# Graph layer and feed-forward block on one core: where the edge keys, the attention rows, the router constants and a comparison table are placed

## The chip, the cores and the metric

The kernel runs on one core of a Trainium2 chip. The metric is the device time of one execution in microseconds (us); lower is better. The core has five engines that each take their instructions in order: PE (matrix multiply; PEld is its weight load), DVE (vectors), ACT (activations and copies), POOL (GpSimd) and SP (which here only issues transfers). Transfers are issued by SP, ACT and POOL, and a transfer that has to wait holds up what stands behind it on its issuing engine.

## The reference

The inputs are x of 1250 nodes by 768, and 41250 edges (src, dst), sorted by dst, with one loop edge for each node among them. Cut to what matters:

```python
n_nodes = x.shape[0]
loops = jnp.arange(n_nodes)
src = jnp.concatenate([edge_index[0], loops]); dst = jnp.concatenate([edge_index[1], loops])

def _gat_layer(x, W, a_src, a_dst, b, src, dst, n_nodes):
    h = x @ W
    e = leaky_relu((h @ a_src)[src] + (h @ a_dst)[dst], 0.2)
    m = segment_max(e, dst);  w = exp(e - m[dst]);  z = segment_sum(w, dst)
    alpha = w / z[dst]
    return segment_sum(h[src] * alpha[:, None], dst) + b

x = x + gat2(relu(gat1(layernorm(x))))
y = layernorm(x)                       # then a feed-forward block:
y = y + attention(ln(y))               # 12 heads of 64, over 1250 rows
x = x + y + moe(ln(y))                 # 8 experts, the best 2 for each row
```

## The kernel before

The kernel turns the edges into a dense matrix of counts, `cnt` (how often the edge from node s to node d occurs), so that a graph layer becomes matrix products over 10 tiles of 125 nodes. It goes through these stages: edge lists and the first layer's projection (to 72 us), counting (to 136 us), two graph layers, attention over 12 heads, the output projection with the router, and the experts.

**The edge lists.** The 41250 edges lie as 125 rows of 330. Their lists `ri` are loaded, and DVE makes one number of each edge, `key` = dst * 1250 + src. The keys are stored to memory (`keys`, with a short `tail` behind them), because the next steps gather from there by computed rows. From the first key of each row, `find_rows` works out in which row each node's edges begin (`begun` on DVE, ten small products on PE, `row` and `edges` on DVE). For each tile t of 125 nodes, `gather_row(t)` fetches that row of keys for each node (`kr`, an indirect transfer issued by POOL, three buffers: LEAD = 3), and `first_edges(t)` counts on DVE how many keys of it are smaller, which gives the position of the node's first edge, and has POOL gather a window of 64 keys from there (`win`). When all ten windows are there, DVE turns them into node numbers, PE sums how many were found (`psum`) and transposes them (`pl`).

**The tiles of x**, beside the edge lists: `spread(t)` loads a tile where it hasn't been loaded yet (four buffers, so tile t waits until tile t - 4 is transposed; even tiles are issued by SP, odd ones by ACT) and takes its statistics on DVE and the root on ACT; `normal(t)` makes the reciprocal and the offset on DVE and scales the tile on ACT; `columns(t)` transposes it on PE in two halves, which ACT copies to `xnT`. `project` multiplies a tile with the layer's weights `gw` (24 matmuls, then ACT copies `h`). `vector(n)` takes n of the 12 products of `gw` with the attention vectors (`scr`, on DVE; the result is `wa`). The vectors are loaded as rows repeated on all partitions (`rep`). `attention_terms` multiplies `wa` with `xnT` on PE (`pe`).

**What sets the order.** Within `tc.manual_schedule`, PE, DVE and POOL keep the order in which the program writes their instructions; ACT and SP are ordered by the scheduler. Instructions outside of such a block are placed by the scheduler where it finds room, unless `tc.keep_in_program_order` pins them. The router's constants (`beyond`, `used`, `start`, `slot`, `before`, `number`, `ones`; lines 781 to 814) are written after attention, are not pinned, and were placed by it in the first 26 us: `ones` on DVE at 1 us, six instructions on POOL behind the first three row gathers, and the comparison that makes `before` a triangle (L812) on DVE behind tile 3's statistics.

**The queues at the start.** SP issues ri (dst), tiles 0 and 2, and the weights `gw` (L112); ACT issues ri (src), `tail`, tiles 1 and 3, and then the keys' store (L233). Of the eight semaphores that count the transfers of SP and ACT, each is used again by a later transfer, which waits for the earlier one: so the weights' issue waits for tile 0, and the store of the keys for tile 1 and for `key`.

**Counting** (L402 to L413): for each of 25 groups of edge positions, DVE compares the source nodes with the table `lane` (`ohp`) and, five times in all, the targets with the table `upto` (`ohj`); PE multiplies the two, and ACT copies the counts. `upto` is made by an iota on POOL (L252).

## Time and profile before

| | |
|---|---|
| median of 3 runs | 1541.51 us (1534.36 to 1543.46) |
| the profiled execution | 1542.12 us, of which the span is 1540.3 us |
| PE busy | 1454.5 us (94%) |
| DVE busy | 797.8 us (52%) |
| ACT busy | 597.6 us (39%) |
| POOL busy | 431.6 us (28%) |
| the chain that ended last | PE 71%, DVE 9%, issue 8%, DMA 5%, ACT 4%, POOL 2% |

Busy time is an average over stages with different limits. The stage that the change is about takes 72 us of 1540, and in it PE is busy for about half of the time: of three stretches of 20 us from the start, PE works 3.6, 12.2 and 18.0 us. A row of the list of waits names the instruction that stood still, what ended its wait, the total in us, how often, and the longest. A row of the chain is start, length, and what the end of the kernel goes back to at that time; "issue" is time in which nothing that the profile shows was waited for. A row of the timeline is start, busy time, engine, line, operation, output and input. The clock in the stretches is what PE was granted, 1.00 being full.

### The profile page before, as it was taken

What the parts mean: (1) busy time and instruction counts of PE and PEld (TensorE: products, weight loads), DVE (VectorE), ACT (ScalarE), POOL (GpSimd) and SP (SyncE); (2) the same over time, 40 slices, a digit from 0 to 9 for tenths busy, and PEclk for the clock granted to TensorE, in tenths of its full rate; (3) what the DMA queues carried; (4) which work ended last, traced back from release to release, by engine and by line L of the source; (5) the groups of instructions that cost most, each with busy time, mean ns of one, the idle gap of its engine ahead of it and who ended that gap; (6) DMA issues with size and microseconds to landing.
All of it is one profiled execution on the core that took longest, in us unless ns stands there. A gap on an engine that the chain in (4) does not pass through costs nothing.

```text
span 1540.3 us, 15938 instructions
## 1 busy us (share of the span) xinstructions
PE 1454.5 (94%) x5981; PEld 782.3 (51%) x5981; DVE 797.8 (52%) x1285; ACT 597.6 (39%) x950; POOL 431.6 (28%) x287
## 2 busy tenths in 40 slices
PE   3889999999999999999999999999988997799998
PEld 2476655555555555553344444434333665466665
DVE  4698633205326740117877877877888665011111
ACT  3321503202414621215655655655656354212121
POOL 5300000000000002004764664664666222122222
PEclk9956999999999999999999999999999997899999
DMA  6200010000021118940000000000030333755644
GB/s 182 66 1 32 11 72 0 0 11 2 1 81 55 56 44 339 407 176 20 1 21 1 21 0 21 1 21 1 0 101 1 131 119 113 288 169 179 219 153 142
DMA packets 48847, 125.49 MB, mean 81 GB/s; under 512 B 6103, under 2 KB 22680, under 8 KB 48768
## 3 DMA queue, kind: packets, MB, share of 16 engines
q1 hardware_dynamic: 30540, 55.04, 10.8%
q0 software_dynamic: 12688, 57.10, 9.8%
q10 hardware_dynamic: 5540, 12.31, 2.7%
q8 instruction: 48, 0.79, 0.2%
q14 instruction: 31, 0.25, 0.1%
HBM read 71.30 MB, written 57.60 MB: 84 GB/s over the span
## 4 chain that ended last, share of the span: by engine, by line
PE 71%; DVE 9%; issue 8%; DMA 5%; ACT 4%; POOL 2%; POOLq 0%; SPq 0%; ACTq 0%; DVEq 0%
PE pagg L525 12%; PE ph L201 9%; PE st L659 8%; PE pav L703 7%; PE pk L622 5%; PE pv L638 5%; PE phe L988 5%; PE poe L997 5%; PE pq L622 4%; DMA xd<-yn,slot 2%; DVE sT L689 2%; PE pc L409 2%; PE pe L190 2%; PE po L846 2%; PE ptr L140 1%
## 5 line engine op out<-in xcount | busy, mean ns | idle before, releaser
L695 POOL TENSOR_TENSOR acc<-acc,sT 125x834 f32<-125x834 f32 (+1 forms) x139 | 272.9, 1963 | 10.9
L525 PE MATMUL pagg<-h,wt 125*125 125x385 f32 (+1 forms) x800 | 262.7, 486 | 0.4 <-DVE wt L518 0.4
L668 DVE TENSOR_TENSOR most<-most,st 125x834 f32<-125x834 f32 (+1 forms) x144 | 147.0, 1021 | 105.3 <-ACT sT L662 101.9
L525 PEld LDWEIGHTS pagg<-h,wt 125*125 125x125 f32 x800 | 147.5, 187 | 106.0 <-DVE wt L518 2.7
L689 DVE TENSOR_TENSOR sT<-sT,mb 125x834 f32<-125x834 f32 (+1 forms) x180 | 174.1, 1016 | 22.9 <-PE mb L684 22.9
L690 ACT ACTIVATE sT<-sT 125x834 f32<-125x834 f32 (+1 forms) x180 | 158.4, 900 | 49.8 <-DVE sT L689 49.4
L662 ACT COPY sT<-st 125x834 f32<-125x834 f32 (+1 forms) x180 | 151.5, 847 | 51.4 <-PE st L659 46.4
L659 PE MATMUL st<-qk 64*125 64x417 f32 (+1 forms) x720 | 164.5, 556 | 3.9 <-DVE most L668 3.8
L703 PE MATMUL pav<-sT,v 125*64 125x417 f32 (+1 forms) x720 | 151.1, 532 | 9.3 <-ACT sT L690 9.3
L600 POOL MEMSET zero<- 128x772 f32 x1 | 0.7, 741 | 519.2 <-PE ptr L140 519.2
L695 POOL TENSOR_TENSOR acc<-sT 125x834 f32<-125x834 f32 (+1 forms) x18 | 35.3, 1963 | 276.0 <-ACT sT L690 276.0
L659 PEld LDWEIGHTS st<-qk 64*125 64x125 f32 x720 | 56.6, 184 | 99.1 <-DVE most L668 42.9
L703 PEld LDWEIGHTS pav<-sT,v 125*64 125x64 f32 x720 | 42.5, 136 | 106.0 <-issue 44.5
L997 PE MATMUL poe<-we,hT 128*128 128x384 f32 x264 | 88.8, 486 | 0.0
L622 PE MATMUL pq<-yT,wqk 128*128 128x417 f32 (+1 forms) x216 | 88.1, 534 | 0.0
L846 PE MATMUL po<-wp,aT 128*125 128x384 f32 x240 | 87.5, 498 | 0.0
L988 PE MATMUL phe<-xT,we 128*128 128x384 f32 (+1 forms) x288 | 86.6, 460 | 0.0
L1001 DVE SCALAR_TENSOR_TENSOR sofar<-poe,weight,sofar 128x768 f32<-128x768 f32 x25 | 25.4, 1018 | 116.3 <-PE poe L997 116.2
L622 PE MATMUL pk<-yT,wqk 128*128 128x417 f32 (+1 forms) x216 | 84.0, 526 | 0.0
L201 PE MATMUL ph<-gw,xnT 128*125 128x384 f32 x240 | 82.6, 504 | 0.0
L638 PE MATMUL pv<-wv,yT 128*125 128x384 f32 x240 | 79.9, 490 | 1.4 <-issue 1.4
L201 PE MATMUL ph<-gw,x1T 128*125 128x384 f32 x240 | 78.6, 487 | 0.0
(219 smaller groups left out, 1734.6 us busy)
## 6 DMA issues: line engine op xcount, KB each, us to landing
xd<-zero POOLq DMA_DIRECT2D x8, 3860.0 KB, 47.4
we<-in_L_ffn_W_dram SPq DMA_DIRECT2D x16, 1152.0 KB
xr<-xd SPq DMA_DIRECT2D x25, 386.0 KB
gw<-in_L_gnn_W_dram SPq DMA_DIRECT2D x2, 2304.0 KB
wqk<-in_L_ffn_Wqkv_dram SPq DMA_DIRECT2D x12, 384.0 KB
xres<-in_x_dram SPq DMA_DIRECT2D x10, 375.0 KB
xsd<-xres ACTq DMA_DIRECT2D x10, 375.0 KB
wv<-in_L_ffn_Wqkv_dram SPq DMA_DIRECT2D x1, 2304.0 KB
```

The costliest lines, as they stand in the source:

```text
L201: nc.tensor.matmul(po[:, s, :DH], xT[:, c, t * T:(t + 1) * T], w[:, c, s * DH:(s + 1) * DH], start=(c == 0), stop=(c == DC - 1))
L525: nc.tensor.matmul(po[:, s, :DH + s], ws[j][:, (d - d0) * T:(d - d0 + 1) * T], h[:, j, s * DH:(s + 1) * DH + s], start=(j == 0), stop=(j = ...
L622: nc.tensor.matmul(pq[:, :w], wqk[:, c, i, :], yT[:, c, c0:c0 + w], start=(c == 0), stop=(c == DC - 1))
L638: nc.tensor.matmul(pv[:T, s, :DH], yT[:, c, t * T:(t + 1) * T], wv[:, c, s * DH:(s + 1) * DH], start=(c == 0), stop=(c == DC - 1))
L659: nc.tensor.matmul(st[:T, i, :w], self.qk[r, 1, j * T:(j + 1) * T], self.qk[r, 0, self.c0:self.c0 + w], start=True, stop=True)
L662: nc.scalar.copy(s[:, :, :w], st[:T, :, :w])
L689: nc.vector.tensor_tensor(s[:, :, :w], s[:, :, :w], self.mb[:T, :, :w], ALU.subtract)
L690: nc.scalar.activation(s[:, :, :w], s[:, :, :w], AF.Exp)
L695: nc.gpsimd.tensor_tensor(self.acc[:, :, :w], prev[:, :, :w], s[:, :, :w], ALU.add)
L703: nc.tensor.matmul(self.pav[r, :w], v[:, j, hd0:hd0 + HD], s[:, i, :w], start=(j == 0), stop=(j == NT - 1))
L988: nc.tensor.matmul(ph[:, :n * P], w1[:, c, f * P:(f + 1) * P], xT[:, c, :n * P], start=(c == 0), stop=(c == DC - 1))
L997: nc.tensor.matmul(po[:, d, :DH], hT[:, f, s * P:(s + 1) * P], w2[:, f, d * DH:(d + 1) * DH], start=(f == 0), stop=(f == FC - 1))
```

## The change

Five edits:

1. **The keys' store** is issued by SP, pinned in program order between the x tiles and the weights; the weights' load stands behind it (and is written out, without the helper `load_big_weight`).
2. **The rows of attention vectors** of the first layer are issued by SP, and a first `vector(1)` at the head of the manual schedule issues both without taking a product: they stand right behind the weights. The second layer's rows stay on ACT.
3. **The tiles** 4 to 9 are spread, normalized and transposed one step of the loop later: `spread(t + 2)` for t from 2 to 7 in place of `spread(t + 3)` for t from 1 to 6, and the spread comes ahead of `first_edges(t)`. So between the first and the second projection PE transposes one tile (was two), between the second and the third three, and after the third two (was one).
4. **The table `upto`** is made by POOL after the first three row gathers, not ahead of them.
5. **The router's constants** are pinned to their place in the program, after attention: the six POOL instructions stand ahead of the memsets of `yn`, and `ones` and `before` on DVE after the last division of attention. `tail` and the odd tiles of x stay on ACT.

On SP's queue the order is now: ri, tiles 0 and 2, keys, weights, two rows, tiles 4, 6, 8.

```diff
@@ attention_vectors
             def load(a):
                 rep = pool.tile([P, D], F32, tag="rep", name="rep", bufs=bufs)
-                tc.keep_in_program_order(nc.scalar.dma_start(
+                tc.keep_in_program_order((nc.sync if bufs > 1 else nc.scalar).dma_start(
                     rep, bass.AP(tensor=a.tensor, offset=a.offset, ap=[[0, P], [1, D]])))
                 return rep
 
             reps = [load(a) for a in (a_src, a_dst)[:bufs]]
+            if bufs > 1:
+                yield None
@@ edge lists
-            gw = load_big_weight(gW1, "gw1")
...
-            nc.scalar.dma_start(keys[0:E].rearrange("(p e) -> p e", p=T), key)
+            tc.keep_in_program_order(nc.sync.dma_start(keys[0:E].rearrange("(p e) -> p e", p=T), key))
+            gw = wpool.tile([P, DC, D], F32, tag="w", name="gw1")
+            tc.keep_in_program_order(nc.sync.dma_start(gw, gW1.rearrange("(c p) f -> p c f", p=P)))
...
             upto = ep.tile([P, 2 * NT, 5 * PG], BF16, name="upto")
-            nc.gpsimd.iota(upto, pattern=[[1, 2 * NT], [0, 5 * PG]], base=1, channel_multiplier=0,
-                           allow_small_or_imprecise_dtypes=True)
...
             with tc.manual_schedule(engines=fixed):
+                vector(1)
                 pk = find_rows()
...
                 for t in range(LEAD):
                     gather_row(t)
+                nc.gpsimd.iota(upto, pattern=[[1, 2 * NT], [0, 5 * PG]], base=1, channel_multiplier=0,
+                               allow_small_or_imprecise_dtypes=True)
...
                 for t in range(NT):
+                    if 2 <= t <= 7:
+                        spread(t + 2)
                     first_edges(t)
                     if t + LEAD < NT:
                         gather_row(t + LEAD)
                     if t % 3 == 0 and t // 3 < EARLY:
                         project(xT, gw, h, gpo, [t // 3])
-                    if 0 < t <= 6:
-                        spread(t + 3)
                     vector(0 if t < 3 else 1 if t < 5 else 2)
-                    if 0 < t <= 6:
-                        normal(t + 3)
-                        columns(t + 3)
+                    if 2 <= t <= 7:
+                        normal(t + 2)
+                        columns(t + 2)
@@ router constants
+    pin = tc.keep_in_program_order
...
-    nc.gpsimd.iota(beyond, pattern=[[REG, NE], [P, NR]], base=CAP - NOWHERE, channel_multiplier=0,
-                   allow_small_or_imprecise_dtypes=True)
+    pin(nc.gpsimd.iota(beyond, pattern=[[REG, NE], [P, NR]], base=CAP - NOWHERE, channel_multiplier=0,
+                   allow_small_or_imprecise_dtypes=True))
...
-    nc.gpsimd.iota(before, pattern=[[1, T]], base=0, channel_multiplier=-1,
-                   allow_small_or_imprecise_dtypes=True)
-    nc.vector.tensor_scalar(before, before, 0.0, None, ALU.is_gt)
+    pin(nc.gpsimd.iota(before, pattern=[[1, T]], base=0, channel_multiplier=-1,
+                   allow_small_or_imprecise_dtypes=True))
+    pin(nc.vector.tensor_scalar(before, before, 0.0, None, ALU.is_gt))
...
```

## The prediction

> **What bounds the kernel now.** I read the page first: PE is busy for 94% of the span and the chain that ended last is PE for 71% of it. The diff touches three places: the edge lists in the first 72 us, the counting loop that reads the table `upto`, and the router 1200 us later. From 78 us on the kernels issue the same instructions in the same order except for eight small ones near the router, so I looked for what ends last in the first 72 us. First the list of waits for 0 to 130 us (engine, line and operation, what ended the wait: total us, times, longest):
>
> ```profile
> POOL kr L278 <- issue: 12.8, 10, 10.2
> PE ptr L140 <- ACT xnT L298: 12.4, 5, 10.2
> ...
> ACT xn L319 <- DVE less L318: 11.3, 6, 8.6
> ...
> DVE before L812 <- POOL before L810: 9.2, 1, 9.2
> ...
> DVE good L374 <- PE psum L372: 4.1, 1, 4.1
> DVE scr L181 <- DMA rep<-in_L_gnn_att_src_dram: 4.1, 1, 4.1
> ```
>
> Four engines stand still at one time, for 9 to 10 us. The chain, in order of time (start us, us, what), says why:
>
> ```profile
> 9.81 9.59 DMA keys<-key
> 19.44 0.97 issue
> 20.41 1.38 POOL kr L278
> ...
> 25.61 0.20 POOL before L810
> 25.83 0.23 DVE before L812
> 26.06 0.08 DVE rstd L316
> 26.17 0.17 DVE less L318
> 26.36 1.03 ACT xn L319
> ...
> 31.59 8.68 PE ph L201 x24
> ...
> 63.02 8.56 PE pe L190 x24
> 71.58 0.33 PE psum L372 x2
> 71.94 0.17 DVE good L374
> ```
>
> The keys' store takes 9.59 us; POOL's three row gathers wait for it; the router's iota `before` stands behind the gathers on POOL; DVE, in order, waits for that iota with tile 3's rstd behind it; ACT can't scale the tile, PE can't transpose it. A router constant holds up the graph layer. PE then runs without a long gap from 31.4 to 71.5.
>
> The timeline shows one more thing at the start:
>
> ```profile
> 7.69 2.51 POOL L252 IOTA upto<- 128x2500 bf16 x1
> ...
> 8.29 1.98 DVE L243 TENSOR_SCALAR node<-node 125x10 f32<-125x10 f32 x1
> ```
>
> A 125x10 operation took 1.98 us beside the iota; `row`, of the same shape, took 0.17. The Trainium skill's "SBUF — State Buffer", "Who interferes with whom", says that a GpSimd operation and a VectorE tensor_scalar in a two-port mode lock each other out, whole instructions at a time; this pair looks like it, and by it all of the 1.8 us would go.
>
> **Step 1, router constants out of the way** (tiles and lists are counted from 0). DVE loses the wait of 9.2 us. Tile 3's variance is done at 16.5 (stats from 15.19, 1.02 + 0.21), ACT's root follows by 16.9, rstd and less by 17.2; ACT scales tile 2 from 16.79 to 17.82 and can scale tile 3 at 17.85, not 26.36: 8.5 us earlier. With `upto` gone from 7.69, `node` costs 0.17 and `begun` about 0.98 (twice the 0.49 of jf, 128x625), so both end near 9.45, not 10.92. The x tile that the statistics wait for is there by 9.47 (the weights' issue waits for the same tile, and went then). So these come 0 to 1.3 us earlier; I take 1.0. The first projection starts at 31.4 - 9.5 = 21.9.
>
> What hid behind the stall is the weights' load. It was issued at 9.47; the transfer rate stands at 362 to 417 GB/s from 12 to 17 us and falls at 17.5, so it ended near 17.8. Now the issue comes about 0.4 us later (one SP issue more), with 165 KB of keys ahead and 3 x 165 KB of gathers beside it, 1.6 us at 400 GB/s: it lands near 19.8. That is 2 us of cover; each microsecond past 21.9 would cost one.
>
> **Step 2, the keys.** The store moves from ACT, where it followed the weights' issue by 0.34 us, to SP ahead of them. It waits there for the key (8.05) and the first x tile, so it goes at about 9.5. Its landing is not in the trace: at best 2.9 us after the issue (the shortest landing of any gather of these lists), at worst 9.6, as before. I take 4 us, near the low end: the first x tiles are nearly through (1.57 MB of 1.87 MB moved by 9.0), and 165 KB need 1.3 us at the 131 GB/s with which the 125-row loads at 140 to 146 us run. So POOL starts the first gather at 9.5 + 4 + 1.0 (its lag in the chain) = 14.5. Gathers landed 3.9 to 7.6 us after their start, median 4.3; beside the weights I take 5.5. Call F the time at which DVE can begin on the first list: F = 20.0, within 17.3 (9.5 + 2.9 + 1.0 + 3.9) and 27.7 (9.5 + 9.6 + 1.0 + 7.6).
>
> A rule speaks against this step. The Trainium skill's "DMA: Bandwidth & Descriptors", "Queues, rings and completion order", says each DMA engine alternates between queues packet by packet. By it the store on ACT's queue needn't have waited for the weights on SP's, and would now take as long: F would be 26. The 9.59 us, 1.5 us past the weights' end, look like a queue in order, and I go by them.
>
> **Step 3, the loop over edge lists.** DVE takes it in order. From F it has two lists, then a tile's statistics (1.27), list (0.68), up to two attention products (0.98 each), rstd and less (0.28) in turn. Gather t+3 starts behind the window gather t (1.5 us each on POOL) and lands 4.3 us later, so list 3 stands at F + 7.9 and list 6 at F + 18.3; tile 8 is normal at F + 21.6, and ACT has scaled it at F + 22.7. `upto` (2.51) now sits on POOL between the third gather (done near 19) and the first window gather, due at F + 0.7 = 20.7; that is nearly free, 0.8 us late at worst here. The rows of attention vectors, issued right behind the weights, remove DVE's 4.1 us for `rep`. That wait wasn't on the path (DVE itself waited 4.1 us for psum at the end).
>
> **Step 4, what is late next.** The lead of the x tiles drops by one: between the first and second projection stands one tile's transposes, not two, and tile 9's load can be issued only after the second projection. With the first projection's start S = 21.9, that one ends at S + 17.3 (8.7 + 0.8 + 7.8). ACT then copies h (0.8), evicts tile 5, scales tile 8 (1.03), evicts tile 6 and issues the load in two parts around tile 7, done near S + 22.8. Before, it was issued at 43.83 and 45.68, S + 14. It lands 2.5 to 3.8 us later (a tile waited for at 34.3 had its issue end at 30.5): S + 26. From its statistics to the last product DVE needs 9.0 us (51.29 to 62.32 before, less two products that now stand earlier): S + 35. The last of six terms and the second chunk's six follow, 0.71 each: S + 40. That equals PE's own 40.1 us (31.4 to 71.5), so the tail uses up its slack and costs 0 to 1. ACT's turn for tile 8 ends at S + 20.2. If list 6 is late, F + 22.7 passes that and all of this moves; that is so when F passes 19.4, and F = 20.0 costs 0.6.
>
> **Step 5, constants at the router.** Two DVE instructions (0.17 + 0.23) come after the last division at 1201.6; DVE idles 1.02 us at 1208.09 for po, which takes them. POOL's six (1.1 together) come before a memset at 1193.3, and POOL idles 4.2 us after it. Nothing; uncovered, 0.4 and 1.1. The load and rows on SP delay no one: SP's next x tile waits for PE at 16.5 anyway.
>
> **Sum.** psum now starts at 71.5; then at 21.9 + 40.1 + 0.6 + 0.4 = 63.0: 8.5 us. The order after that is the same, so it stays to the end. The profiled execution took 1542.1 (span 1540.3 and 1.8 around it), close to the median of the runs, 1541.5: 1542.1 - 8.5 = **1533.6**.
>
> **The rivals.**
> *The gathers take the wait over* (0.22). If the store stays slow or gathers are starved, F = 23 to 27, and psum starts at about F + 42.5 (22.7, and the 19.8 from S + 20.2 to S + 40). For: the store's own 9.59 us beside the weights. Against: it is now ahead of them. Gain 2 to 6: 1536 to 1540.
> *The change doesn't do what it says* (0.08). The weights land after 29, or the order of queues means nothing: gain under 2, 1540 to 1542.
> *Slower* (0.06): the first gather, on POOL's queue, lands only after weights and attention rows and tiles, past 29.0 us, where F + 42.5 passes 71.5. One microsecond each; at 34 it makes 1547. Against it: weights, rows, keys, gathers and the rest of the tiles are 4.1 MB, done by 22 us at 400 GB/s.
> *More* (0.08): PE's clock, 0.50 from 76 to 144 us, drops in PE's wait at 73 to 79. With a warm PE the counting stage (58.7 us) is left to DVE's 25 x 1.90 + 5 x 1.46 = 54.8: another 3.9, 1529 to 1530. The same wait remains, so I doubt it.
>
> **How the numbers follow.** My forecast has 0.56, 7 to 10 us. The three runs before spread over 9 us, so the median of the runs after may lie 4 off on its own. From the largest gain (10) less 5 for that, the range reaches down to 1526; up to 1542 it takes in the first two rivals. A measurement of this kernel tells about 1% (15.4 us) from no change. No case here reaches that alone; forecast and *more* with a lucky median give faster 0.10, the slower rival with an unlucky one slower 0.05, within 1% 0.85.
>
> **What would show it.** In the new profile: no wait of DVE for `before` in the first 72 us; `node` near 0.2 us; the first gather at 14 to 15 and the first list at 18 to 22; projection one at 21 to 23; psum at 62 to 65. Wrong: a keys landing still near 19; projection one waiting for the weights; DVE standing for kr or for x tile 9 by more than 6 us; a different clock in the counting stage.

## The result, and the profile after

The changed kernel takes 1539.82 us in the median of 14 runs (1537.19 to 1541.68), the kernel before 1542.26 us in 14 runs taken beside it (1534.36 to 1543.98): ratio 0.9989, 95% interval 0.9979 to 0.9999. Some 2 us came (2.4 by the medians, 1.7 by the ratio), where 8.5 were forecast. The profiled execution took 1540.10 us with a span of 1538.3 us.

The chain, in order of time (start us, us, what):

```profile
15.59 12.19 DMA xn<-in_x_dram
27.80 1.03 DVE st L119 x2
...
32.96 5.36 DMA kr<-keys,row
38.34 0.58 DVE key L286 x2
...
46.69 1.51 PE ptr L140 x6
48.20 9.69 PE ph L203 x24
57.91 0.69 ACT h L206
58.61 0.85 ACT xnT L299 x2
59.46 0.93 ACT xn L320
...
61.54 10.26 PE pe L192 x24
71.80 0.33 PE psum L376 x2
```

The stall on the router constant is gone, and psum starts where it did: 71.8 us (71.5 before). So the 2 us lie behind psum: in the two profiles 1.0 us between psum and the first layer's `pmx`, transposes behind the counting (91.1 us before, 90.1 after; the clock stands at 0.50 there from 74.3 to 146.0 us before, from 75.9 to 144.1 after), 0.4 from there to the router's last `prk` (a product that counts rows for the experts), and 0.8 from there to the end. The sum of the prediction has no term for them, and no run below explains them. In the stall's place stand a transfer of x tile 4 that takes 12.2 us, a gather of 5.4 us, and three PE and ACT steps that are longer than before: the third projection 9.7 us (7.9), the scaling of tile 9 behind the copy of h, and the attention terms 10.3 us (8.6).

The waits of 0 to 130 us (engine, line and operation, what ended them: total us, times, longest) say the same:

```profile
DVE key L286 <- DMA kr<-keys,row: 11.5, 4, 8.0
...
PE ptr L140 <- ACT xnT L299: 7.2, 4, 3.6
...
DVE st L119 <- DMA xn<-in_x_dram: 6.7, 2, 5.7
POOL kr L279 <- DVE less L319: 6.7, 1, 6.7
DVE good L378 <- PE psum L376: 6.5, 1, 6.5
...
PE ptr L140 <- ACT xn L320: 3.8, 2, 1.9
```

DVE waits 8.0 us for the first row of keys and 5.7 us for x tile 9. PE waits 7.2 us in all for ACT's copies of tiles that are transposed already, and 3.8 for tiles that ACT has not scaled. The longest of the former, 3.6 us, ends with copies that stand in ACT's order behind the scaling of the next tile, which waited 2.8 us for DVE's `less`.

Two tables of stretches (from:to, length, then busy us of PE, PEld, DVE, ACT and POOL with counts, granted clock, share of the DMA engines' time, GB/s). First the transfers, before and then after:

```profile
12.00:18.00 6.00, 2.57 (x11) 1.73 (x11) 4.31 (x18) 4.26 (x8) 0.00 (x0) 1.00 0.93 359
18.00:24.00 6.00, 0.00 (x0) 0.00 (x0) 0.00 (x0) 0.00 (x0) 3.05 (x4) 1.00 0.33 107
24.00:28.00 4.00, 0.20 (x1) 0.20 (x2) 2.06 (x10) 1.64 (x3) 2.52 (x8) 1.00 0.30 84
```

```profile
12.00:18.00 6.00, 2.61 (x10) 1.86 (x11) 3.42 (x16) 5.53 (x10) 2.95 (x4) 1.00 1.01 398
18.00:24.00 6.00, 6.00 (x24) 4.13 (x24) 0.12 (x1) 2.44 (x6) 3.46 (x2) 1.00 1.04 275
24.00:28.00 4.00, 4.00 (x14) 2.33 (x13) 1.51 (x7) 0.00 (x0) 2.41 (x2) 1.00 0.77 183
```

Before, the gathers of 20 to 26 us had the DMA engines nearly to themselves (share 0.33). After, weights, rows, gathers and tiles fill them until 26 us, and at full share they move only 275 GB/s from 18 to 24 us. Then PE's clock, after:

```profile
40.00:46.00 6.00, 1.24 (x10) 0.71 (x7) 5.02 (x16) 3.51 (x6) 5.08 (x4) 0.93 0.23 60
46.00:52.00 6.00, 5.31 (x13) 3.47 (x14) 1.02 (x2) 1.95 (x5) 1.20 (x2) 0.50 0.37 106
52.00:62.00 10.00, 7.84 (x33) 4.61 (x32) 7.85 (x24) 3.61 (x7) 4.93 (x3) 1.00 0.05 10
62.00:66.00 4.00, 4.00 (x8) 0.73 (x6) 3.47 (x6) 0.00 (x0) 0.00 (x0) 0.57 0.00 0
```

PE works 1.2 of the 6 us ahead of the third projection, and gets half its clock in the 6 us after; once more at 62 us. In stretches of 0.2 us the two spells at 0.50 reach from 45.2 to 52.0 and from 62.2 to 65.6 us. Before, the record shows 1.00 from the start to 74 us.

### The profile page after: what moved, and what is told of

It reads as the page before. It is cut to its first block, busy times and chain, and to the rows that moved or that the text cites. A ratio compares the mean times of both kernels' runs of the same rounds, so it can differ in the third digit from the quotient of the medians.

```text
span 1538.3 us, 15938 instructions
## 1 busy us (share of the span) xinstructions
PE 1457.0 (95%) x5981; PEld 782.8 (51%) x5981; DVE 796.7 (52%) x1285; ACT 597.8 (39%) x950; POOL 433.9 (28%) x287
## 3 DMA queue, kind: packets, MB, share of 16 engines
q1 hardware_dynamic: 30958, 55.99, 10.8%
## 4 chain that ended last, share of the span: by engine, by line
PE 70%; DVE 11%; issue 8%; DMA 5%; ACT 4%; POOL 1%; SPq 0%; POOLq 0%; DVEq 0%; ACTq 0%
PE pagg L529 12%; PE ph L203 8%; PE st L663 8%; PE pav L707 7%; PE pk L626 5%; PE pv L642 5%; PE phe L993 5%; PE poe L1002 5%; PE pq L626 4%; DVE sT L693 2%; DMA xd<-yn,slot 2%; PE pe L192 2%; PE pc L413 2%; PE po L851 2%; DMA xn<-in_x_dram 1%
## 5 line engine op out<-in xcount | busy, mean ns | idle before, releaser
L693 DVE TENSOR_TENSOR sT<-sT,mb 125x834 f32<-125x834 f32 (+1 forms) x180 | 174.2, 1016 | 22.6 <-PE mb L688 22.6
L699 POOL TENSOR_TENSOR acc<-sT 125x834 f32<-125x834 f32 (+1 forms) x18 | 35.4, 1965 | 275.2 <-ACT sT L694 275.2
```

Source lines behind the costliest of these rows:

```text
L693: nc.vector.tensor_tensor(s[:, :, :w], s[:, :, :w], self.mb[:T, :, :w], ALU.subtract)
L699: nc.gpsimd.tensor_tensor(self.acc[:, :, :w], prev[:, :, :w], s[:, :, :w], ALU.add)
```

## The experiments

17 kernels were run. The mark that tells most is the start of psum, since the instructions behind it are the same; the whole time follows it within some 4 us. "First list" is when DVE begins on the first row of keys (the prediction's F); tiles and lists are counted from 0. All have the new loop order unless "old loop" is said. "Held" means that idle matmuls keep PE's clock up. Each mark is from one profiled execution. The six kernels that do not differ up to the first list (changed, r2, r4, r6, r7, r10) have it at 23.3 to 25.5, and r6 and r7, which do not differ up to psum, have that at 69.3 and 68.9; so a difference of 1 to 2 us between two rows shows nothing by itself. Times in us; the last columns give the median and the ratio to the kernel before, run beside it, with its 95% interval.

| kernel | first list | tile 6's statistics | psum | from tile 6 to psum | median | ratio |
|---|---|---|---|---|---|---|
| before (old loop) | 26.3 | 37.2 | 71.5 | 34.3 | 1541.2 to 1542.4 | |
| changed | 23.9 | 32.8 | 71.7 | 38.9 | 1539.8 | 0.9989 (0.9979 to 0.9999) |
| r3 pins alone, old loop | 27.1 | 35.4 | 70.3 | 34.8 | 1540.8 | 0.9988 (0.9977 to 0.9999) |
| r8 all but rows and loop | 24.7 | 33.4 | 68.4 | 35.0 | 1537.9 | 0.9970 (0.9951 to 0.9990) |
| r2 all but the loop | 23.5 | 32.2 | 68.6 | 36.4 | 1538.2 | 0.9975 (0.9964 to 0.9987) |
| r1 constant rows | 23.9 | 34.2 | 70.2 | 36.0 | not compared | |
| r4 held | 25.5 | 34.9 | 67.7 | 32.9 | 1534.0 | 0.9950 (0.9933 to 0.9967) |
| r10 old loop, held | 25.0 | 33.8 | 68.9 | 35.1 | 1535.4 | 0.9953 (0.9938 to 0.9968) |
| r6 old loop, second projection earlier, held in part | 23.3 | 33.1 | 69.3 | 36.2 | 1535.7 | 0.9950 (0.9934 to 0.9967) |
| r5 weights and rows behind the gathers | 20.3 | 40.6 | 80.5 | 39.9 | 1548.9 | 1.0049 (1.0034 to 1.0064) |
| r9 weights first, old loop | 26.6 | 36.3 | 70.2 | 33.9 | 1541.3 | 0.9987 (0.9977 to 0.9997) |
| r11 weights first, old loop, held | 26.5 | 35.9 | 73.7 | 37.9 | 1539.5 | 0.9981 (0.9971 to 0.9990) |
| r12 weights first, held | 26.8 | 37.8 | 71.4 | 33.6 | 1538.9 | 0.9979 (0.9969 to 0.9989) |
| r14 weights cut in two | 19.2 | 34.6 | 70.6 | 35.9 | 1542.3 | 1.0004 (0.9994 to 1.0013) |
| r13 weights cut, held | 19.5 | 34.9 | 67.9 | 33.1 | 1536.3 | 0.9964 (0.9950 to 0.9978) |
| r15 rows late, held | 22.6 | 33.4 | 65.8 | 32.4 | **1533.3** | 0.9945 (0.9928 to 0.9961) |
| r16 rows late, weights cut, held | 19.9 | 37.6 | 70.0 | 32.4 | 1539.5 | 0.9978 (0.9968 to 0.9988) |

The two that are not in the table are r7 (the counting stage) and r17 (a control).

### What each edit gives: r3, r2

r3 is the kernel before with the `pin(...)` lines of the router alone.

> The kernel before with the router's constants pinned behind attention, and nothing else. Theory (the wait for the gathers takes the place of the wait for the router's comparison): the first projection starts at 22.5 to 23.5, 8.5 us earlier; the first gather still at 20.4, the first list at 24 to 26.3; psum at 69 to 72, so at most 2.5 us of the 8.5 arrive. Rival (the comparison was the stall, all else has room): psum at 63.

psum at 70.3, 1.2 us earlier: the stall goes and the next wait stands right behind it. DVE now waits 9.8 us for the first row of keys, whose gather starts at 19.7 (20.4 before):

```profile
POOL kr L278 <- issue: 12.1, 10, 9.4
...
DVE key L285 <- DMA kr<-keys,row: 11.6, 2, 9.8
```

r2 is the changed kernel with its loop put back:

```diff
                 for t in range(NT):
-                    if 2 <= t <= 7:
-                        spread(t + 2)
                     first_edges(t)
...
+                    if 0 < t <= 6:
+                        spread(t + 3)
                     vector(0 if t < 3 else 1 if t < 5 else 2)
-                    if 2 <= t <= 7:
-                        normal(t + 2)
-                        columns(t + 2)
+                    if 0 < t <= 6:
+                        normal(t + 3)
+                        columns(t + 3)
```

> The changed kernel with the loop's order as before: tile t + 3 in step t, for t from 1 to 6, behind the first list of the step. Theory (the late gather is the first cause, the shorter lead of the tiles the second): first list still at 23.9; tile 9's load is issued before 38 us, not at 45 to 48; PE waits longer ahead of the third projection; psum at 68 to 70.5. Rival (the shorter lead alone takes the gain back): psum at 62 to 64. If the order does not matter: 71 to 72.

psum at 68.6 and 1538.2 us: in these profiles the four other edits are worth 2.9 us at psum, and the loop takes 3.1 back (1.6 in the whole time, where the intervals overlap). Tile 9 is scaled at 47.5 (59.3 in the changed kernel), with no wait of DVE for it. But both later projections run cold, at a clock of 0.50, for 3.4 us (9.60 us each, 7.91 at full clock):

```profile
34.89 0.91 PE L140 MATMUL ptr<-ident,xn 125*128 125x125 f32 x6 [3.90 <-ACT xnT L299]
35.64 9.60 PE L203 MATMUL ph<-gw,xnT 128*125 128x384 f32 x24
...
49.27 9.60 PE L203 MATMUL ph<-gw,xnT 128*125 128x384 f32 x24
```

### Rows or weights: r1, r8, r5

```diff
-                tc.keep_in_program_order((nc.sync if bufs > 1 else nc.scalar).dma_start(
-                    rep, bass.AP(tensor=a.tensor, offset=a.offset, ap=[[0, P], [1, D]])))
+                nc.gpsimd.memset(rep, 0.03)  # the first layer's two rows only
```

r1 replaces the two row loads by constants, made on POOL. The attention of layer 1 is then another, and with it all values behind it and the rows that each expert gets, so only the first 72 us are compared.

> The changed kernel without the two loads of attention rows behind the weights: the rows are filled with a constant on POOL instead (two memsets ahead of the first gather), so the first layer's attention is not the reference's. Nothing else moves. Theory (the rows hold up the gathers and x tile 4 on the transfer engines): the first list begins on DVE at 20 to 21.5 us, not 23.9; tile 4's statistics at 22 to 25, not 27.8; psum starts at 66 to 69, not 71.8. Rival (the weights alone hold the gathers up): first list still at 23 or later, psum at 71 or later.

The first list did not move (23.94): the rows do not hold the first gather. What is left ahead of it are the weights, which r5 and r13 move. The second list came at 24.6 (27.1) and tile 4's statistics at 25.3 (27.8): these the rows do hold. And psum gained only 1.5 us of it, which is no more than the scatter.

r8 is the kernel before with the keys, the table and the pins; rows and loop are as before.

> The kernel before with three of the change's edits: keys stored on SP ahead of the weights, the table moved behind the gathers, the router constants pinned; the rows of attention vectors stay on ACT and the loop keeps its lead of three. Against the run with the old loop order it differs in the rows alone. Theory (the rows' move is worth little, since they are ready long before the psum either way; they delay tile 4's load by 2 to 3 us where they are early): first list 23 to 24, tile 4's statistics at 25 to 26 and not 27, psum 67 to 69.5, time within 0.1% of that run (1537 to 1539). Rival (the rows' move was a part worth having): DVE waits for them 3 us or more on the path and psum comes at 70 or later.

psum at 68.4, 0.2 us from the run with the rows moved (r2): no gain of the rows' move is seen. Without it DVE waits 4.8 us for them, and list 1 comes at 25.5 in place of 26.4: the two sides cancel.

r5 asks the other way round, with weights and rows on POOL's queue behind the first three gathers:

```diff
-            tc.keep_in_program_order(nc.sync.dma_start(gw, gW1.rearrange("(c p) f -> p c f", p=P)))
...
                 for t in range(LEAD):
                     gather_row(t)
+                nc.gpsimd.dma_start(gw, gW1.rearrange("(c p) f -> p c f", p=P))
+                vector(1)                    # the rows, on POOL too
```

> The changed kernel, with the first layer's weights and the two rows of attention vectors loaded from POOL's queue behind the first three row gathers, not from SP's queue ahead of them; nothing is left out. Question: why is the first list late (23.88 us, its gather issued at 14.50 and landed 9.4 us later)? Theory (the weights' transfer holds the gathers on the shared DMA engines, as the run without the rows hinted): with the weights behind them the first gather lands 4 to 6 us after its start, so the first list starts at 18.5 to 21, near the 20.0 of the prediction; the first projection then waits for the weights and starts at 23 to 26. Rival (the gather itself is slow this early, by its reading of keys just stored or by POOL's own work): the first list still starts at 23 or later. The sum at psum is not told apart by it: 66 to 72 us, since the order of the tiles and the PE clock stay as they are.

The first list at 20.26, 6.1 us after the start of its gather (9.4 in the changed kernel), near the 5.5 that the prediction had. The second and third follow at once, at 20.9 and 22.9. The price, from the chain:

```profile
18.57 15.10 DMA gw<-in_L_gnn_W_dram
...
33.71 11.01 PE ph L203 x24
```

The weights land 15 us after their issue, PE waits 12.1 us for them, and the kernel is 7.8 us slower than the one before, by the medians. Whoever stands behind pays.

### The clock: r4, r10, r6, r7

r4 is the changed kernel with idle matmuls (a product of `xnT` and `gw` that nobody reads) in PE's waits, 4 behind the transposes of tile 5, 2 behind those of tiles 6 and 8:

```diff
+            def keep_warm(n):
+                pd = epc.tile([P, 512], F32, tag="pc", name="pwarm")
+                for i in range(n):
+                    nc.tensor.matmul(pd[:T, :DH], xT[:, 0, 0:T], gw[:, 0, 0:DH], start=True, stop=True)
```

> The changed kernel with eight more products on PE in its waits (four after tile 5's transposes, two after tile 6's, two after tile 8's; their results go nowhere). Theory (of what was lost, 3.7 us are PE's clock at half after its waits): the third projection takes 7.9 us, not 9.9, the attention terms 8.6, not 10.3; the clock stays at 1.00 from 40 to 74 us; psum at 68 to 69. Rival (the clock only fills time in which DVE or ACT would be waited for): psum at 71 or later.

psum at 67.7 and 1534.0 us, though the lists came 1.7 us later in this profile. The clock holds, and with it the third projection and the terms have their durations of before:

```profile
48.52 7.91 PE L203 MATMUL ph<-gw,xnT 128*125 128x384 f32 x24
...
59.24 8.56 PE L192 MATMUL pe<-xnT,wa 128*2 128x417 f32 x24 [0.24 <-ACT xnT L299]
67.74 0.38 PE L385 MATMUL psum<-found,ones 125*128 125x1 f32 x2
```

```profile
46.00:52.00 6.00, 5.46 (x21) 3.13 (x20) 1.90 (x9) 2.90 (x6) 2.28 (x2) 1.00 0.40 122
```

Tile 9 is now scaled at 54.4, before the third copy of h and not behind it. So ACT's late turn for tile 9 in the changed kernel was a consequence of the other delays, not a cost by itself. The idle matmuls are the only edit, the medians differ by 5.8 us (1539.8 and 1534.0), and the intervals of the ratios are apart.

r10 puts idle matmuls into the old loop, before the transposes of tiles 5 to 8:

```diff
+                    if 1 < t < 6:
+                        keep_warm(4 if t == 2 else 2)
                     if 0 < t <= 6:
                         normal(t + 3)
```

> The changed kernel with the old loop order, and with idle matmuls (4 before the transposes of tile 5, 2 before those of tiles 6, 7 and 8) to hold PE's clock; the projections stay where that order has them. Theory (in the old order the clock at half speed is what is left: both later projections took 9.60 us, 7.91 at full clock, and the last one waited for the one before): projections of 7.9 to 8.2 each, granted clock 1.00 from 20 to 70, tile 9 scaled by 46.5, psum 64.5 to 66.5 (68.63 without the idle matmuls). Rival (PE waits for ACT's turns and DVE's lists, so a faster PE only waits longer): psum 67.5 to 69.

A miss: the two later projections took 7.91 us each, as expected, and psum did not move (68.9; 68.6 in r2), as the rival says. In the old loop PE waits for tiles and copies either way. With the clock held, neither loop is shown to be the better one: psum at 67.7 and 68.9, 1534.0 and 1535.4 us, and the intervals overlap.

r6 has the second projection between tiles 4 and 5 in the old loop, with pairs of idle matmuls:

```diff
-                    if t % 3 == 0 and t // 3 < EARLY:
-                        project(xT, gw, h, gpo, [t // 3])
+                    if t in (0, 2, 6):
+                        project(xT, gw, h, gpo, [(t + 1) // 3])
+                    if 2 < t < 6:
+                        keep_warm(2)
```

> The changed kernel with three edits: the lead of the x tiles back to three (as in the run with the old loop order), the second projection put between the transposes of tiles 4 and 5, and pairs of idle matmuls between the transposes of tiles 5 to 8 to hold PE's clock. Theory (of the 8.8 us missing at psum, the tile order and the cold clock are some 5.5, the late first list the rest, and this last matters only while the tile order makes the end follow DVE): the first list stays at 23.5 to 25.5, the projections take 7.9 to 8.2 each at a granted clock of 1.00, tile 9 is scaled before 47, psum at 61.5 to 65 (changed kernel 71.73, old loop order 68.63), and the whole time is 1531 to 1535. Rival (the end follows the first list, as the prediction's step 3 had it, at 44 us after it): psum stays at 67 or later whatever PE does, the time at 1536 or more.

A miss too: psum at 69.3. Tile 5 was transposed later, so tile 9 was loaded later (DVE waited 4.4 us for it), and the pairs were too few: the clock was 0.50 from 46.4 to 49.8 us, though no projection stood in that.

r7 adds idle matmuls to r6, around the counting. It tests the prediction's rival *more*.

```diff
+                keep_warm(16)
                 for g in range(NP // PG):
...
                     if g % 4 == 3:
                         next(terms, None)
+                    else:
+                        keep_warm(2)
```

> The kernel of the last run, with idle matmuls added in PE's wait before the counting stage (16) and two in each counting group that has no attention product. Theory (the clock of 0.50 in the counting stage comes from PE's waits, and a warm PE leaves the stage to DVE): granted clock 1.00 from 20 to 150 us, the stage from its first to its last matmul group 54 to 56 us in place of 58.7, and the clock needs no recovery in the second layer's projection behind it (another 2 to 3 us): 5 to 7 us less than the last run, 1525 to 1530. Rival (the clock falls in this stage whatever stands in the waits, because the small matmuls themselves count as little work): clock 0.50 again, the added matmuls cost 0.66 us each pair at that clock, and the stage is as long or up to 10 us longer.

Neither. The clock stood at 1.00 for nearly all of the stage, and the kernel took 1559.7 us (ratio 1.0110, 1.0094 to 1.0127). From the groups of instructions (line, engine, operation, tiles, shapes, count, then busy us and mean ns), the counting matmul and the attention terms of this stage in the changed kernel, at a clock of 0.50:

```profile
L413 PE MATMUL pc<-ohj,ohp 128*128 128x20 bf16 x625 | 45.2, 221 | 9.5 <-DVE ohp L409 9.2
...
L192 PE MATMUL pe<-xnT,wa 128*2 128x416 f32 x12 | 9.3, 876 | 0.0
```

and in this one, at 1.00 for nearly all of the stage:

```profile
L421 PE MATMUL pc<-ohj,ohp 128*128 128x20 bf16 x594 | 42.8, 220 | 0.0
L334 PE MATMUL pwarm<-gw,xnT 128*125 128x384 f32 x84 | 34.2, 537 | 0.0
...
L192 PE MATMUL pe<-xnT,wa 128*2 128x416 f32 x10 | 4.3, 512 | 0.0
```

221 and 220 ns: these matmuls, with 170 ns of weight load each, gain nothing from the clock, while the terms beside them do (876 and 512 ns). The stage can't be won this way, and the idle matmuls are paid for: each pair took 1.5 us of PE.

### First things first: r9, r11, r12

These issue the weights on SP right behind x tile 0, at 2 us in place of 10: r9 in the old loop, r11 held in the old loop, r12 held in the new one.

```diff
                 xrows.append(xn)
+                if t == 0:
+                    gw = wpool.tile([P, DC, D], F32, tag="w", name="gw1")
+                    tc.keep_in_program_order(nc.sync.dma_start(gw, gW1.rearrange("(c p) f -> p c f", p=P)))
```

> The changed kernel with the old loop order (lead of three), and with the weights' load issued on SP right behind x tile 0, ahead of tile 2, of the keys and of all gathers (at about 2 us, not 10). Nothing is left out. Theory (the first list is late because the weights move at the same time as its gather, and psum follows the first list one for one): the weights are through by 15, the first gather starts at 14.5 to 17 and lands 4 to 6 us later, the first list starts at 19 to 22 (23.53 without this edit), the first projection at 21 to 23.5, and psum comes 1.5 to 4 us before the 68.63 of the run without it: 64.6 to 67.1. Rival (the bytes are the same and something else gives way): x tiles 2 and 3 or the keys' store come late by as much, the first list is at 23 or later or the first projection at 24 or later, and psum stays at 68 or more.

> Both edits of the two runs above in one kernel: old loop order, weights' load behind x tile 0, idle matmuls. Theory (late first list, tile order and clock are the three terms that the prediction missed, and they add): first list 19 to 22, projections at full clock, psum 61 to 64.5, near the 63.0 of the prediction; time 1530 to 1534. Rival (the terms hide one another): no earlier than the better of the two runs above by more than 1 us.

> The changed kernel with its own loop order, its idle matmuls as in the run that held the clock, and the weights' load behind x tile 0. Theory (there psum followed the first list at 42.2 us after it: 25.54 and 67.74): first list 19 to 22, psum 61.5 to 65. Rival (the load of tile 9 and ACT's turn set the end in this order, whatever the list): tile 9's statistics still at 49 or later, psum 66.5 to 68.

The rivals were right in r9 and r11. In r12 neither was: with the first list at 26.8 and tile 9's statistics at 53.4, psum came at 71.4. In r9's chain x tile 2, issued behind the weights, lands 13.3 us later, and the keys, issued at 10.47, land so late that the first gather starts at 22.3 (14.5 in the changed kernel):

```profile
6.75 13.27 DMA xn<-in_x_dram
20.11 1.03 DVE st L119 x2
...
22.32 0.90 POOL kr L280
```

### Both terms put right: r13, r14, r15, r16, r17

r13 cuts the weights' load by columns. The half that the first twelve matmuls need stays behind the keys; x tile 4, the other half and the rows follow. r14 is the same without idle matmuls.

```diff
-            tc.keep_in_program_order(nc.sync.dma_start(gw, gW1.rearrange("(c p) f -> p c f", p=P)))
+            gwv = gW1.rearrange("(c p) f -> p c f", p=P)
+            tc.keep_in_program_order(nc.sync.dma_start(gw[:, :, :DH], gwv[:, :, :DH]))
...
+                xrows.append(xn)             # x tile 4, loaded here, on SP
+                tc.keep_in_program_order(nc.sync.dma_start(gw[:, :, DH:], gwv[:, :, DH:]))
+                vector(1)                    # the rows
```

> The changed kernel with its own loop order and idle matmuls to hold the clock, and with the weights' load on SP cut in two by columns: the half that the first twelve matmuls need stays behind the keys, then x tile 4, then the other half, then the rows of attention vectors. Nothing is left out. Theory (two terms of the prediction were wrong, the first gather's landing and PE's clock, and with both put right its sum holds): the first gather starts at 14.5 to 15.5 and lands 5 to 7 us later, the first list at 19.5 to 22, the first projection still at 21 to 23, granted clock 1.00 to 70 us, psum 42 to 43 us after the first list, so at 61.5 to 65 (63.0 was predicted; 71.73 in the changed kernel, 67.74 with the clock held alone), time 1528 to 1533. Rival (the bytes of the half, and of what follows, hold the gather or PE as much as before): the first list at 23 or later, or PE waits for the second half inside the first projection beyond 33, and psum stays at 67 or later.

> The same cut of the weights' load in the changed kernel without the idle matmuls. Theory: the first list at 19.5 to 22 as in the run above, but PE's clock falls to 0.50 in its waits for tiles 7 to 9, and psum stays 45 to 48 us behind the first list: 65 to 69. Rival (the clock fell only because the first list came late and PE had to wait for tiles): the clock stays at 1.00 to 70 us and psum comes at 61.5 to 65 without idle matmuls.

The first list came at 19.5 and the first projection at 20.9, near the prediction's 20.0 and 21.9, and psum stayed at 67.9. DVE's timeline in r13 (in brackets: idle time before it, and what ended it) shows why:

```profile
19.49 0.56 DVE L287 SCALAR_TENSOR_TENSOR key<-kr,node,ones 125x330 f32<-125x330 f32 x1 [3.99 <-DMA kr<-keys,row]
...
28.11 0.56 DVE L287 SCALAR_TENSOR_TENSOR key<-kr,node,ones 125x330 f32<-125x330 f32 x1 [7.86 <-DMA kr<-keys,row]
```

The second list is as late as ever: its gather starts at 15.95, between the issues of the second half (15.61) and of the rows (16.04 and 16.64), and takes until 28.1. psum does not follow the first list, as my theory had it, but the lists and tiles that come after 27 us. Without the idle matmuls (r14) psum is 2.6 us later, at 70.6 and so beyond its range too, with a third projection of 9.97 us, and the median is 6.0 us higher: after the changed kernel and r4, this is the second pair that differs in the idle matmuls alone and whose intervals are apart.

r15 leaves the weights whole and puts the rows behind the loads of x tiles 4 and 6; r16 cuts the weights as well, with the second half behind x tile 4.

```diff
-                vector(1)
                 pk = find_rows()
...
                 for t in range(4):
                     columns(t)
+                for t in range(4, 7):
+                    xn = op.tile([T, D], F32, tag="xn", name="xn", bufs=4)
...
+                    xrows.append(xn)
+                vector(1)                    # the rows
```

> The changed kernel with idle matmuls to hold the clock, and with the two rows of attention vectors behind the loads of x tiles 4 and 6 on SP, not right behind the weights. Nothing is left out. Theory, reformed by the runs with the cut load (psum follows tile 4's statistics, which need the second list and x tile 4, and not the first list: 38.9 and 39.2 us after them with the clock held, 43 to 45 without; the rows keep both until 27 to 29): tile 4's statistics at 25 to 26.5, psum at 64 to 65.5, time 1530 to 1533. Rival (with the rows gone from 16 to 27 us something else fills it, or the rows are then late for DVE): tile 4's statistics at 27.5 or later, or a wait of DVE for rep above 2 us, and psum at 66.5 or later.

> The run above with the weights' load cut in two as well: the second half behind x tile 4 on SP, the rows behind x tile 6. Theory: first list at 19.5 to 20.5, the second half is through by 25.5 and PE hardly waits for it, tile 4's statistics at 23 to 25, psum 39 us after them, at 62 to 64.5: the prediction's 63.0 reached, time 1528 to 1532. Rival (the second half takes the rows' place ahead of the second list): tile 4's statistics at 26 or later and psum at 65 or later, no better than the run above.

r15 has tile 4's statistics at 23.9, psum at 65.8 and 1533.3 us, the lowest median: 8 us under the kernel before, 6.5 under the changed one, and not told from r4 by the intervals. psum is 0.3 us outside of its range, although tile 4's statistics came earlier than theirs: DVE waited 3.8 us for list 3, whose gather ran beside the rows. From tile 4's statistics to psum it took 41.9 us, not 39, so psum doesn't follow them either. In r16 the second half of the weights did what the rival says: PE waited 4.3 us for it, tile 6's statistics came at 37.6.

r17 is a control, made from the kernel before:

```diff
                 for t in range(4):
+                    if t == 3:
+                        keep_warm(8)
                     columns(t)
```

> The kernel before with eight idle matmuls (16 as the trace counts them) in PE's wait of 10.2 us ahead of tile 3's transposes: a control for the runs with idle matmuls. Theory (there the clock never fell in the first 72 us, so there is nothing to hold): first projection, psum and whole time as before, within 0.1%; the 1 to 2 us that the runs with idle matmuls win behind the first layer come from elsewhere. Rival (more matmuls early are worth something by themselves, in whatever place): 2 to 4 us less than before.

It took 1546.0 us (1.0023, 1.0014 to 1.0033), 4.3 us more than before, and it doesn't control what it should: the idle matmuls waited for ACT's copies with everything else and ran after the stall, not in it, so that 6.3 us of them stood on the path (psum came 6.9 us later). It shows something else. The first projection took 8.88 us in the kernel before and 7.91 here, behind the idle matmuls (first the kernel before, then r17):

```profile
31.38 8.88 PE L201 MATMUL ph<-gw,xnT 128*125 128x384 f32 x24
```

```profile
29.42 6.29 PE L333 MATMUL pwarm<-gw,xnT 128*125 128x384 f32 x16
35.55 0.81 PE L140 MATMUL ptr<-ident,xn 125*128 125x125 f32 x6
36.19 7.91 PE L201 MATMUL ph<-gw,xnT 128*125 128x384 f32 x24
```

Both stand at a recorded clock of 1.00. So the theory's "there the clock never fell" read too much out of the record: a 1.00 ahead of the first recorded fall does not show a full clock. That the clock was low there is the likely reading of the durations; no record here shows it.

## Why the prediction was wrong

The first half was right, item by item: no wait for `before` in the first 72 us; `node` 0.17 us (1.98); the keys' store at 9.05 (9.5), the first gather at 14.50 (14.5, hit exactly by two errors that cancel: the store went 0.45 us earlier and, by the prediction's own lag of 1.0 us, landed some 4.4 us after its issue, not 4), the first projection at 21.3 (21.9); nothing lost at the router, where the stretch from the first layer's `pmx` to the router's first product takes 1048.9 us (1049.2). The page on "SBUF — State Buffer" was borne out: with the iota moved, `node` lost all of its 1.8 us.

psum came at 71.7, not 63.0. By the prediction's own steps tile 6's statistics should have come at F + 9.8 (list 3 at F + 7.9, then the list, a product, rstd and less: 0.68 + 0.98 + 0.28), so at 29.8, and psum 33.2 us later (63.0 less 29.8; the prediction did not state this difference). The five kernels with this loop and idle matmuls have 32.4 to 33.6 us between the two. This part of step 3 and step 4 was right, as long as PE has its clock. The missing 8.7 us are two terms:

**Step 2, the landing of the gathers: 3.0 us.** Tile 6's statistics came at 32.8. The store landed nearly as I said, but the first gather took 9.4 us and not 5.5, and x tile 4, which step 3 took for granted, landed 12.2 us after its issue. Step 5's "The load and rows on SP delay no one" was wrong for both: with the weights behind the gathers (r5) or halved (r13) the first list stands at 20.3 and 19.5, and without the rows (r1) tile 4's statistics at 25.3 (27.8). The estimate in the rival *slower*, "4.1 MB, done by 22 us at 400 GB/s", was wrong too: from 18 to 24 us full engines moved 275 GB/s, from 24 to 28 us 183 at a share of 0.77. The rival *the gathers take the wait over* had the place and a good price for F (23 to 27); its time for psum, F + 42.5, was still 5 us early. The Trainium skill's "DMA: Bandwidth & Descriptors", "Queues, rings and completion order", has a second rule that I passed over: a transfer's completion mark lands only after every earlier write of the same DMA engine, across its queues. The rows here agree with it in part: the first gather, on POOL's queue, lands 9.4 us after its start with the weights ahead on SP's, and 6.1 with the weights behind it (r5). But the weights were there by 21.3, when the projection started, and the gather landed at 23.9, so the weights alone don't give that time, and no run tells this rule from a plain sharing of the engines.

**Step 4, PE's own time: 5.7 us, most of it PE's clock.** "PE's own 40.1 us" was taken from a profile in which PE waited 0.7 us at most at a time after 31 us. The changed kernel leaves PE waits of 3.6 and 1.8 us between 40 and 47 us and of 1.9 us at 58.5; the clock stood at 0.50 from 45.2 to 52.0 and from 62.2 to 65.6, the third projection took 2.0 us more, the terms 1.7, and tile 9 was scaled behind the late copy of h. I had the clock only in the rival *more*, for the stage after. r4 shows the term: 38.9 us from tile 6 to psum become 32.9, by idle matmuls alone. Nearly 1 of these 6.0 us comes ahead of the fall at 45.2, though (tile 7 is scaled 8.45 us after tile 6's statistics in the changed kernel, 7.50 in r4), so the clock's share is nearer to 5. Nor is it a fixed price: r1 and r14, with the same loop and no idle matmuls, have one spell at 0.50 behind tile 6's statistics, not two, and 36 us to psum. And it isn't the new loop alone: once the stall is gone the old loop has such spells too (second projection 9.2 to 9.6 us in r3, r8 and r2). The Trainium skill's "TensorE: Matmul & The Clock Gate", "Part 1", speaks of a fall after a window of about 3.4 us without work. The wait of 3.6 us is as long as that, though the clock fell only 1.2 us after its end. r2's second fall, at 49.4 us behind waits of 0.6, 0.2 and 0.8 us, does not fit the rule. The 10.2 us wait of the kernel before fits it by the 8.9 us of the projection behind it, and not by the record, which stays at 1.00.

The rivals: the time, 1539.8, lies at the border of two. *The gathers take the wait over* (1536 to 1540) has the mechanism of the first term and knows nothing of the second, and since the 2 us lie behind psum, its number is luck. *The change doesn't do what it says* (gain under 2) is near it for a wrong reason, since the change does. *Slower* did not come; r5, which is slower, is not that mechanism, since there the gathers land early and the weights late. *More* can't come at all: the counting matmuls last 221 ns at 0.50 and 220 at 1.00.

What stays open: the kernels with idle matmuls win some 1.5 us more between the router and the end than the place of psum explains (from the last `prk` to the end 234.2 to 237.1 us, without them 236.8 to 237.8); r17, meant to separate this, did not. The pairs r10 and r2, r11 and r9 show the same from the other side: the median is 2.8 and 1.8 us lower with idle matmuls, and psum no earlier, though the intervals overlap. Nor is it known why the first gather takes 9.4 us and not 6 behind weights that have landed, or why full DMA engines move 400 GB/s before 18 us and 275 after; the kernel without rows has 259 there.

## What to carry to other kernels

A stall hides what runs beside it: before its removal is priced, list every transfer that was done in its shadow, and ask what each will now be waited for, the second and third as much as the first. A stage's own time is valid only for the waits it had; where an edit makes PE wait a few microseconds in a stage of long matmuls, price the half clock behind it (here some 1.7 us for each spell of 3.4 us that PE works through), and fill the wait with idle matmuls only where PE really stands in it. An order of loads is a matter of who pays: each reordering here (weights first, weights last, weights halved) moved the wait to another transfer. Moving back the load that nobody needed soon, the rows (r15), brought tile 4's statistics 3 to 5 us forward and gave the lowest median, and even that is not told from r4 in the whole time.

## What the runs showed of the hardware

- A 161 KB store issued 0.34 us behind 2.3 MB of weights on another queue took 9.6 us (before); ahead of them, some 4.4 us (changed, from its issue to 1 us before the first gather); 8 us behind them on the same queue, some 10.8 us (r9, reckoned in the same way).
- The counting matmul (128x20, bf16, a new weight load for each) takes 221 ns at a granted clock of 0.50 and 220 at 1.00, the attention terms of the same stage (128x416, fp32) 876 and 512 ns; the projections' 24 matmuls took 7.9 us at full clock and 9.2 to 10.1 us when the record shows a fall in part of them.
- Every spell at a clock of 0.50 that begins and ends in the first 72 us lasts 3.4 us or two or three times that: 6.8 and 3.4 us in the changed kernel, 3.4 twice in r2, 10.2 in r1. One of 3.4 us that PE works through costs 1.7 us: the terms took 10.26 us for 8.56 in the changed kernel, the later projections of r2 9.60 for 7.91.
- The clock's record can stand at 1.00 while the matmuls are slow: the first projection took 8.88 us (before), 9.04 (r4) and 11.0 (r5, behind a wait of 12.1 us) ahead of any recorded fall, and 7.91 in r17 behind idle matmuls.
- In r7, with PE busy without a gap from 71 to 155 us, the clock nevertheless fell to 0.50 for 3.4 us at 104, 128 and 152 us.
